# Row 0's Sinkhorn chains: reciprocals as a power of minus one on GpSimd

## The chip, the cores and the metric

The kernel runs on one core of one Trainium2 chip. A core has five engines that each execute their own list of instructions strictly in order: PE (matrix multiply), DVE (VectorE), ACT (ScalarE), POOL (GpSimd) and SP, which here only issues DMAs. They meet through semaphores. The metric is the device time of one execution in microseconds (us). Three runs of the kernel before gave 1398.83, 1407.75 and 1408.99 us; the median is 1407.75 us.

## The reference, cut to what matters

The model has two layers on an input of 2 batch rows of 512 tokens and 512 channels. Layer 0 is a gated linear attention and a feed-forward product, layer 1 a softmax attention and a mixing of four streams per token. The change touches only that last part. For every token a 4x4 matrix is made doubly stochastic by 50 Sinkhorn steps, which the reference does on logarithms:

```python
def sinkhorn_log(logits, num_iters=50, tau=0.1):
    Z = logits / tau
    u0 = jnp.zeros(Z.shape[:-1], Z.dtype)
    v0 = jnp.zeros_like(u0)
    def step(carry, _):
        u, v = carry
        u = -jax.nn.logsumexp(Z + v[..., None, :], axis=-1)
        v = -jax.nn.logsumexp(Z + u[..., :, None], axis=-2)
        return ((u, v), None)
    (u, v), _ = jax.lax.scan(step, (u0, v0), None, length=num_iters)
    return jnp.exp(Z + u[..., :, None] + v[..., None, :])
...
x_pre = jnp.einsum('btnc,btn->btc', x_streams, H_pre)
y = x_pre @ W_branch
x_mixed = jnp.einsum('btij,btjc->btic', H_res, x_streams)
y_distributed = jnp.einsum('btc,btn->btnc', y, H_post)
return (x_mixed + y_distributed).reshape(B, T, nC)
```

`H_res` is the result of `sinkhorn_log`, blended with the identity. A batch row ("row 0", "row 1") is one of the two entries of the first axis.

## The kernel before

The tokens stand 128 to a tile, so each batch row has four tiles. The first 1000 us or so are layer 0. Layer 1's attention (`maxima`, `weigh`, `outputs`, `finish`) follows in pieces of one kind after another; each finished pair of query tiles is handed to `streams(b, c0, n, last, ways)`, which does the final mixing for n = 2 tiles. There are four such calls. In the order of their start they are called A and B here (batch row 0, first and second half) and C and D (batch row 1). `last` is the entry of the constant `VECTOR = False, False, True, True`: it is false for A and B, true for C and D.

`streams` is a generator. After the norms and the small logits it carves its variables for the Sinkhorn steps out of one tile named `sinkhorn` (128 x 512): `z`, `K` and `t` hold two 4x4 matrices per partition (128 x 32), `fa` and `fb` the row and column factors (128 x 8). The first step is done with logarithms, the other 49 (`range(1, NITER)`) in plain numbers: multiply `K` by one factor (L1120 or L1124), add along one axis (`sums`), take the reciprocal (L1122 or L1126). One multiplication, sum and reciprocal is called a half-step here; a chain has 98 of them, each waiting for the one before. After steps 16 and 32 the factors are folded into the logarithms and `K` is formed anew with two Ln and one Exp on ACT and four additions on DVE.

Where `last` is true, all three operations are on DVE (`big = nc.vector`, one reduction in L1109). Where it is false, the multiplication is on POOL and the sum is two additions on POOL (L1112 and L1113, four to two to one); only the reciprocal is on DVE. So a half-step of A or B goes from POOL to DVE and back.

When a chain is done, DVE forms `hr` (L1135 to L1139) and each of the two tiles is mixed in one of three ways (`WAYS`): "tensor" (ACT makes diagonal matrices, PE multiplies, L1160 and L1161, DVE scales in L1165, POOL adds the residual in L1181), "gpsimd" (B's second tile: L1168, L1172, L1176, L1180, L1181 all on POOL) or "vector" (D's first tile, on DVE). A DMA then stores the tile.

The order of the instructions on each engine is fixed before the kernel runs. The source is traced in the order of the pieces; `aside(2)` advances each live `streams` generator by two `yield`s per piece, with a raised priority (`UPS`, 400). A planner then gives every engine its list from these priorities and from its own estimates of when an instruction will be ready. On the chip nothing is reordered: if the next instruction of an engine has to wait, all behind it wait too. POOL's list holds, beside the chains A and B, the attention's last two operations `o` and `xres` (L930, L932), which `streams` of the same tiles wait for. DVE's list holds the attention's maxima (L847) and the chains C and D beside the reciprocals of A and B.

Of the kernel before, what the change touches and what calls it, by code (L numbers as in the profile page):

```python
# [33 lines left out]
ALU = mybir.AluOpType  # L34
# [19 lines left out]
def tile_adaln(ctx: ExitStack, tc: tile.TileContext, a: dict, out: bass.AP):  # L54
    nc = tc.nc
# [11 lines left out]
    def act(o, i, func, **kw):  # L67
        ins = nc.scalar.activation(o, i, func, **kw)  # L68
        tc.add_manual_dep(
            ins.ins, table.ins.name,  # L70
            mybir.DependencyInfo(mybir.DependencyClass.NoSync, mybir.DependencyReason.DATA),
            reason="the activation table",
        )
        return ins.ins
# [80 lines left out]
    def bank(shape, name, bufs=2):  # L155
        return psp.tile(shape, FP, name=name, bufs=bufs)
# [810 lines left out]
    def streams(b, c0, n, last, ways):  # L967
# [87 lines left out]
        sh, sv = [P, n, NS, NS], [P, n, NS]  # L1055
# [6 lines left out]
        def carve(shape):  # L1062
            m = int(np.prod(shape[1:]))
            t = room[:, used[0]:used[0] + m]
            used[0] += m
            if len(shape) == 4:
                return t.rearrange("p (c i j) -> p c i j", i=NS, j=shape[3])
            return t.rearrange("p (c i) -> p c i", i=NS)
# [24 lines left out]
        fa, fb, fl = carve(sv), carve(sv), carve(sv)  # L1093
# [4 lines left out]
        def kernel_of():  # L1098
            nc.vector.tensor_tensor(K, z, over(u), ALU.add)
            nc.vector.tensor_tensor(K, K, along(v), ALU.add)  # L1100
            act(K, K, AF.Exp)
# [4 lines left out]
        def sums(dst, y):  # L1106

            if last:
                nc.vector.tensor_reduce(dst, y, AX.X, ALU.add)  # L1109
            else:  # L1110
                h2 = pairs
                nc.gpsimd.tensor_tensor(h2, y[:, :, :, 0:2], y[:, :, :, 2:4], ALU.add)  # L1112
                nc.gpsimd.tensor_tensor(dst, h2[:, :, :, 0], h2[:, :, :, 1], ALU.add)  # L1113

        fresh = True
        for it in range(1, NITER):
            if fresh:
                sums(fa, K)
            else:
                big.tensor_tensor(t, K, along(fb), ALU.mult)  # L1120
                sums(fa, t)
            nc.vector.reciprocal(fa, fa)  # L1122
            yield
            big.tensor_tensor(t, tp_(K), along(fa), ALU.mult)  # L1124
            sums(fb, t)
            nc.vector.reciprocal(fb, fb)  # L1126
            fresh = it in (16, 32)
            if fresh:
                for d, f in ((u, fa), (v, fb)):
                    act(fl, f, AF.Ln)  # L1130
                    nc.vector.tensor_tensor(d, d, fl, ALU.add)
                kernel_of()
            yield
# [6 lines left out]
        for c in range(n):  # L1140
            f = wts.tile([P, NS, P], FP, name="fout", bufs=2)
            ff = f.rearrange("p i c -> p (i c)")
            hv = h[c].rearrange("p (i c) -> p i c", i=NS)
            f4 = [P, NS, P]
            way = ways[c]
            if way == "vector":
                for i in range(NS):
                    nc.vector.tensor_scalar(f[:, i], yb[:, c, :], sm[:, c, 1, i:i + 1], None, ALU.mult)
                    for j in range(NS):
                        nc.vector.scalar_tensor_tensor(  # L1150
                            f[:, i], hv[:, j], hr[:, c, i, j:j + 1], f[:, i], ALU.mult, ALU.add
                        )
                    yield
            elif way == "tensor":
                mps = bank(f4, "mix")
                for i in range(NS):
                    dg = wts.tile([P, NS + 1, P], FP, name="dg", bufs=2)
                    for j in range(NS + 1):
                        w = hr[:, c, i, j:j + 1] if j < NS else sm[:, c, 1, i:i + 1]
                        nc.scalar.activation(dg[:, j], ident, AF.Copy, scale=w)  # L1160
                        nc.tensor.matmul(  # L1161
                            mps[:, i], lhsT=dg[:, j], rhs=hv[:, j] if j < NS else yb[:, c], start=j == 0, stop=j == NS
                        )
                    yield
                nc.vector.tensor_tensor(ff, mps.rearrange("p i c -> p (i c)"), rows1[b, GB], ALU.mult)  # L1165
            else:
                tj = wts.tile(f4, FP, name="tj", bufs=1)
                nc.gpsimd.tensor_tensor(  # L1168
                    f, yb[:, c, :].unsqueeze(1).to_broadcast(f4), sm[:, c, 1, :].unsqueeze(2).to_broadcast(f4), ALU.mult
                )  # L1170
                for j in range(NS):
                    nc.gpsimd.tensor_tensor(  # L1172
                        tj, hv[:, j].unsqueeze(1).to_broadcast(f4),
                        hr[:, c, :, j].unsqueeze(2).to_broadcast(f4), ALU.mult,
                    )
                    nc.gpsimd.tensor_tensor(f, f, tj, ALU.add)  # L1176
                    yield
            other = nc.vector if way == "vector" else nc.gpsimd
            if way != "tensor":
                other.tensor_tensor(ff, ff, rows1[b, GB], ALU.mult)  # L1180
            other.tensor_tensor(ff, ff, xs[c], ALU.add)  # L1181
            nc.sync.dma_start(out=out[(t0 + c) * P:(t0 + c + 1) * P, :], in_=ff)
            yield

    order = [
        {"b": b, "half": half, "t": t} for b in range(B) for half in range(2) for t in range(4)
# [53 lines left out]
    def weighed():  # L1240
        w = wt[0]
        wt[0] += 1
        if w < n_pieces:
            if w == n_pieces // 2:
                row_tiles(1, (GA,))
                values1(1)
            weigh(order[w // 8], w % 8)
        o = w - OUT
        if 0 <= o < n_pieces and o % 4 == 3:
            outputs(o // 4)  # L1250
        o -= 5
        if o >= 0 and o % 4 == 0 and o < n_pieces:
            j = o // 4
            finish(j)
            if j % 16 == 5:
                with behind():
                    row_tiles(j // 16, (SB, CB, GB))
                    weights24(j // 16)
            if j % 8 == 7:
                side.append((RATES[j // 8], streams(j // 16, j % 16 // 8 * 2, 2, VECTOR[j // 8], WAYS[j // 8]), UPS[j // 8]))  # L1260
# [170 lines left out]
```

## Time and profile before

The profiled execution took 1409.56 us, of which the span from the first to the last instruction is 1407.8 us.

| | busy in the span, us | share |
|---|---|---|
| PE | 1247.3 | 89% |
| DVE | 1164.4 | 83% |
| ACT | 825.1 | 59% |
| POOL | 787.2 | 56% |

| stretch, us from the start | PE busy | DVE busy | POOL busy | what is in it |
|---|---|---|---|---|
| 1111 to 1199 | 79.41 of 88 | 75.60 | 46.82 | attention, chain A |
| 1199 to 1265 | 62.38 of 66 | 55.48 | 39.63 | attention, A and B |
| 1265 to 1300 | 17.00 of 35 | 28.97 | 26.90 | A, B, C; D begins |
| 1300 to 1330 | 0.00 of 30 | 28.20 | 25.56 | all four chains |
| 1330 to 1370 | 11.99 of 40 | 37.51 | 23.89 | B, C, D; A is mixed |
| 1370 to 1390 | 17.45 of 20 | 16.47 | 9.24 | D; B and C are mixed |
| 1390 to 1408 | 7.92 of 18 | 14.63 | 9.24 | D is mixed |

An instruction's duration in these rows contains what it spends in the engine's pipeline, so neighbours on one engine overlap: 0.19 us instructions of DVE start 0.11 us apart where nothing makes them wait. A wait counts as idle time in front of an instruction, with the releaser beside it. A share over the whole span says little here, because the last 150 us have another limit than the rest.

### The profile page before, as it was taken

To read this page: it belongs to the slowest core of one execution; us is meant where nothing else is said; L and a number is where in the kernel's file an instruction comes from. 1 tells how busy PE (TensorE), PEld (TensorE's weight loads), DVE (VectorE), ACT (ScalarE), POOL (GpSimd) and SP (SyncE) were. 2 spreads that over 40 slices of the span, in tenths; PEclk is the share of its full clock that TensorE was granted. 3 is DMA by queue.
4 is the path that set the end of the run, shared out by engine and by line. 5 is a ranking of instruction groups with operands and counts; after the bars stand their busy time and mean duration, and the time that the engine had idled before them with its cause. 6 is when DMAs were issued, how large, how long until landed. Compare 5 with 4: busy or idle time off the path is not lost. (4 is left out here: it accounts for less than half of the span.)

```text
span 1407.8 us, 23038 instructions
## 1 busy us (share of the span) xinstructions
PE 1247.3 (89%) x7128; PEld 990.5 (70%) x7128; DVE 1164.4 (83%) x3171; ACT 825.1 (59%) x2333; POOL 787.2 (56%) x1180
## 2 busy tenths in 40 slices
PE   6979999999999999999988998899998899994117
PEld 3767888788788778888876777677776667762116
DVE  7998668687677687787999977788699879888998
ACT  5456576476476466666665655567567467653226
POOL 4363274365264367577777757644243644657854
PEclk9999999999999999999999999999999899986568
DMA  7121241231131233224333327623212331100001
GB/s 241 36 70 43 87 124 39 68 106 53 53 118 56 94 117 111 81 79 128 120 106 90 98 70 233 179 66 97 65 42 94 101 92 48 59 2 1 1 15 46
DMA packets 95378, 117.14 MB, mean 83 GB/s; under 512 B 10828, under 2 KB 50508, under 8 KB 95256
## 3 DMA queue, kind: packets, MB, share of 16 engines
q1 hardware_dynamic: 95256, 115.67, 27.6%
q8 instruction: 57, 0.93, 0.3%
q14 instruction: 65, 0.53, 0.1%
HBM read 102.11 MB, written 10.64 MB: 80 GB/s over the span
## 5 line engine op out<-in xcount | busy, mean ns | idle before, releaser
L847 DVE TENSOR_REDUCE m<-s 128x1 f32<-128x512 f32 x256 | 166.6, 673 | 21.8 <-PE s L843 21.5
L68 ACT ACTIVATE pt<-s 128x512 f32<-128x512 f32 x256 | 137.4, 601 | 33.1 <-PE s L877 31.5
L448 POOL TENSOR_TENSOR q<-xcos,rot 128x512 f32<-128x512 f32 x64 | 92.8, 1450 | 56.5 <-DVE xcos L446 52.5
L68 ACT ACTIVATE sg<-sg 128x512 f32<-128x512 f32 x128 | 80.7, 632 | 64.5 <-DVE sg L479 62.5
L496 POOL TENSOR_SCALAR_AFFINE_SELECT dec<-gb 128x512 f32<-128x512 f32 x64 | 48.3, 755 | 121.2 <-DMA gb<-g_dram 65.4
L843 PE MATMUL s<-ks,qs 96*128 96x512 f32 x256 | 104.9, 442 | 11.5 <-DVE m L847 7.6
L877 PE MATMUL s<-qs,ks 100*128 100x256 f32 x512 | 104.4, 309 | 10.2 <-DMA qs<-mm 6.8
L233 PE MATMUL pps<-hh,wq_h 128*128 128x512 f32 x256 | 103.3, 403 | 7.1 <-ACT vT L767 3.4
L877 PEld LDWEIGHTS s<-qs,ks 100*128 100x128 f32 x512 | 82.7, 199 | 32.8 <-issue 7.9
L68 ACT ACTIVATE dec<-dec,room 128x128 f32<-128x128 f32 x256 | 83.0, 398 | 34.8 <-POOL dec L496 34.6
L233 PE MATMUL ops<-wo_h,zh 128*128 128x512 f32 x256 | 102.2, 399 | 1.2 <-ACT zh L571 1.0
L233 PE MATMUL gps<-wg_h,hh 128*128 128x512 f32 x256 | 101.3, 398 | 1.5 <-ACT wg_h L210 1.2
L233 PE MATMUL ops<-wo_h,zl 128*128 128x512 f32 x256 | 101.5, 396 | 0.7 <-DVE zl L572 0.7
L233 PE MATMUL pps<-hl,wq_h 128*128 128x512 f32 x256 | 101.8, 398 | 0.0
L233 PE MATMUL pps<-hh,wq_l 128*128 128x512 f32 x256 | 101.5, 397 | 0.0
L233 PE MATMUL gps<-wg_l,hh 128*128 128x512 f32 x256 | 101.1, 395 | 0.0
L233 PE MATMUL ops<-wo_l,zh 128*128 128x512 f32 x256 | 100.6, 393 | 0.0
L233 PE MATMUL gps<-wg_h,hl 128*128 128x512 f32 x256 | 100.6, 393 | 0.0
L516 POOL TENSOR_TENSOR gb<-gb,q 128x512 f32<-128x512 f32 x48 | 62.3, 1299 | 60.3 <-ACT gb L68 46.7
L549 PE MATMUL yps<-v,dec 128*128 128x128 f32 x512 | 93.4, 278 | 2.7 <-DVE xcos L446 1.4
L555 ACT ACTIVATE z<-yps 128x128 f32<-128x128 f32 x256 | 67.5, 278 | 41.1 <-PE yps L551 30.5
L559 DVE SCALAR_TENSOR_TENSOR z<-yps,ss,sg 128x128 f32<-128x128 f32 x256 | 72.0, 340 | 22.5 <-ACT ss L68 22.3
(321 smaller groups left out, 3984.4 us busy)
## 6 DMA issues: line engine op xcount, KB each, us to landing
gb<-g_dram SPq DMA_DIRECT2D x64, 256.0 KB
raw<-in_wq SPq DMA_DIRECT2D x56, 256.0 KB
raw<-in_wg SPq DMA_DIRECT2D x48, 256.0 KB
raw<-in_wo SPq DMA_DIRECT2D x48, 256.0 KB
raw<-in_wmod SPq DMA_DIRECT2D x40, 256.0 KB
qs<-q_dram SPq DMA_DIRECT2D x64, 96.0 KB
q_dram<-hi SPq DMA_DIRECT2D x16, 256.0 KB
raw<-in_wk SPq DMA_DIRECT2D x14, 256.0 KB
```

What stands on the lines that cost most here:

```text
L68: ins = nc.scalar.activation(o, i, func, **kw)
L233: nc.tensor.matmul(ps, lhsT=l, rhs=r, start=i == 0, stop=i == n - 1)
L448: nc.gpsimd.tensor_tensor(dst, sp(xc_), sp(rot), ALU.add)
L496: anchor["pool"] = nc.gpsimd.affine_select(out=dec, in_=gb, pattern=[[0, REP0], [1, P]], compare_op=ALU.is_ge, fill=-1e30, base=0, channel ...
L516: nc.gpsimd.tensor_tensor(gb, gb, q[:, c], ALU.mult)
L549: nc.tensor.matmul(yps[:, h, :], lhsT=u["pr"][:, h, :], rhs=u["v"][:, c, :], start=True, stop=not c)
L555: nc.scalar.activation(z[:, h, :], yps[:, h, :], AF.Square, accum_out=ss[:, h:h + 1])
L559: nc.vector.scalar_tensor_tensor(z[:, h, :], yps[:, h, :], ss[:, h:h + 1], sg[:, h * P:(h + 1) * P], ALU.mult, ALU.mult)
L843: anchor["pe"] = nc.tensor.matmul(ps, lhsT=st["qs"][rp][0:KS, i, qt * P:(qt + 1) * P], rhs=st["ks"][s][0:KS], start=True, stop=True,).ins
L847: anchor["dve"] = nc.vector.tensor_reduce(st["m"][:, 2 * qt + s, i:i + 1], ps, AX.X, ALU.max, negate=True).ins
L877: nc.tensor.matmul(ps[:, j, :], lhsT=st["ks"][s][0:KM, kt * P:(kt + 1) * P], rhs=st["qs"][rp][0:KM, i, :], start=True, stop=True,)
```

## The change

The chains with `last` false (A and B) no longer use DVE for the reciprocal. A constant tile of minus one is written once per `streams` call, and POOL raises the factor, element by element, to that power. The chains C and D keep DVE's reciprocal. Nothing else in the kernel is edited.

```diff
+        minus1 = carve(sv)
+        nc.gpsimd.memset(minus1, -1.0)
+
+        def inverse(f):
+            if last:
+                nc.vector.reciprocal(f, f)
+            else:
+                nc.gpsimd.tensor_tensor(f, f, minus1, ALU.pow)
+
         fresh = True
         for it in range(1, NITER):
...
-            nc.vector.reciprocal(fa, fa)
+            inverse(fa)
             yield
             big.tensor_tensor(t, tp_(K), along(fa), ALU.mult)
             sums(fb, t)
-            nc.vector.reciprocal(fb, fb)
+            inverse(fb)
```

## The prediction

> **What bounds the kernel now.** I read the 40 slices first. In order: PE, DVE, POOL.
>
> ```profile
> PE   6979999999999999999988998899998899994117
> DVE  7998668687677687787999977788699879888998
> POOL 4363274365264367577777757644243644657854
> ```
>
> PE is the limit until about 1270 us; then it falls to 4, 1, 1 and DVE stands at 9. The end of the kernel is the Sinkhorn chains. Next the groups on the tile `sinkhorn` (minimum/median/maximum ns, first and last start):
>
> ```profile
> L1113 POOL TENSOR_TENSOR sinkhorn<-sinkhorn x196: 193/201/686, 1111.6 to 1370.5; 128x8 f32<-128x8 f32 x196
> L1122 DVE RECIPROCAL sinkhorn<-sinkhorn x196: 142/193/204, 1114.1 to 1387.8; 128x8 f32<-128x8 f32 x196
> L1126 DVE RECIPROCAL sinkhorn<-sinkhorn x196: 138/193/204, 1119.4 to 1389.0; 128x8 f32<-128x8 f32 x196
> ```
>
> A and B run on POOL from 1111 to 1370 us, C and D on DVE until 1389. Of 392 reciprocals, the 196 of A and B leave DVE. The timeline (start, duration) gives the pace. POOL, A and B interleaved, then B alone:
>
> ```profile
> 1301.97 0.21 POOL L1112 TENSOR_TENSOR sinkhorn<-sinkhorn 128x16 f32<-128x16 f32 x1
> ...
> 1303.28 0.21 POOL L1112 TENSOR_TENSOR sinkhorn<-sinkhorn 128x16 f32<-128x16 f32 x1
> ```
> ```profile
> 1331.08 0.24 POOL L1120 TENSOR_TENSOR sinkhorn<-sinkhorn 128x32 f32<-128x32 f32 x1 [0.32 <-DVE sinkhorn L1109]
> 1331.40 0.21 POOL L1112 TENSOR_TENSOR sinkhorn<-sinkhorn 128x16 f32<-128x16 f32 x1
> 1331.69 0.20 POOL L1113 TENSOR_TENSOR sinkhorn<-sinkhorn 128x8 f32<-128x8 f32 x1
> 1332.20 0.25 POOL L1124 TENSOR_TENSOR sinkhorn<-sinkhorn 128x32 f32<-128x32 f32 x1 [0.32 <-DVE sinkhorn L1122]
> ```
>
> Interleaved, six instructions (two half-steps) take 1.31 us: 0.65 per half-step, POOL nearly full (17.50 of 20 us busy in 1300 to 1320). Alone, a half-step takes 1.12 us, of which 0.51 passes between the start of the last addition and the next multiplication: 0.20 for the addition, the detour over DVE the rest. Last, DVE with D alone:
>
> ```profile
> 1374.43 0.19 DVE L1109 TENSOR_REDUCE sinkhorn<-sinkhorn 128x8 f32<-128x32 f32 x1
> 1374.65 0.20 DVE L1122 RECIPROCAL sinkhorn<-sinkhorn 128x8 f32<-128x8 f32 x1
> 1374.89 0.21 DVE L1124 TENSOR_TENSOR sinkhorn<-sinkhorn 128x32 f32<-128x32 f32 x1
> 1375.13 0.19 DVE L1109 TENSOR_REDUCE sinkhorn<-sinkhorn 128x8 f32<-128x32 f32 x1
> ```
>
> 0.70 us per half-step. From 1297 (D's start) to 1389, D takes 92 us for 98 half-steps, 0.94 each; the excess is other chains' work on a DVE that is busy 19.39 of 20 us in 1340 to 1360.
>
> **What leaves DVE.** 196 reciprocals at 0.19 us, 37 us of busy time, 0.11 us of pace each. 80 of them (as many as L1113 has there) lie in 1111 to 1265, beside a PE that is the limit (79.41 of 88 us busy until 1199): I give them 0 to 5 us. While D runs, it would fall towards 98 x 0.69 = 68 us, plus 3 us for two new formations of `K` and some 6 us for L1165 and for blocked multiplications: D would end near 1374 instead of 1389. DVE's gain is 15 us, 20 with the attention, if POOL lets it through.
>
> **What is added to POOL.** 196 powers on 128x8 (and four memsets; L828's take 0.13 us, and no one reads those of C and D). No row of this trace shows a power, so I call its time p and bound it. Lower end: the addition of the same shape, L1113, 0.20 us. The additions of 128x32, 128x128 and 128x512 take 0.24, 0.46 and 1.27 us: 2.1 ns per element on a floor of 0.19 us. I suppose that a power is worked out as a logarithm, a product and an exponential, in elementary steps that each cost what an addition does. With 100 of them at 2.1 ns for 8 elements it is 0.19 + 1.68 = 1.9 us, my upper end; the longest single instructions of POOL in this stretch, L211 with 1.73 and L670 with 1.70 us, are close to it. Between 0.2 and 1.9 I take 48 steps, p = 1.0 us: an estimate (two series of a dozen terms each, a multiplication and an addition per term), nearest to the 128x512 row. Below 0.2 nothing: no elementwise row of POOL is shorter at this shape.
>
> **The sum.** POOL's half-step becomes 0.65 + p interleaved. Alone it is 0.32 + 0.29 for multiplication and first addition, 0.29 to the power's start, p, and a 0.09 gap such as stands between dependent instructions above: 1.0 + p. Against 1.12 today, a chain alone is faster only for p under 0.13. So nothing is gained on POOL; only DVE's relief counts.
>
> With p = 1.0: between A's start at 1111 and B's at 1199, POOL has 46.8 us of work, 24.2 of it not the chains'. The remaining 63.8 us hold 63.8/2.0 = 32 half-steps of A, as many as today (L1113 has 32 there: today DVE's waits set the pace).
>
> ```profile
> POOL sinkhorn L1120 <- DVE sinkhorn L1126: 15.4, 15, 2.1
> POOL sinkhorn L1124 <- DVE sinkhorn L1122: 13.9, 13, 3.5
> ```
>
> (Who waits for whom in 1111 to 1265; us, times, longest. These waits are what goes, and p fills the place.) Then 66 half-steps of A beside 66 of B: 132 x 1.65 = 218 us. B's last 32 alone: 64 us. Other work of POOL after 1199 (L930, L932, L956, L1007 and A's L1181): 12 us. B ends at 1199 + 218 + 64 + 12 = 1493 instead of 1370. Then `hr` 1 us, B's second tile on POOL (L1168 1.04, four times 1.05 + 1.27, L1180 1.33, L1181 1.27: 12.9), another L1181, the store 3 us: 19 us with gaps. Span **1512 us**. The profiled execution lies 1.8 us above its span and 1.8 above the median, so the time on the median's scale is also **1512 us**.
>
> In general the end by POOL is 1294 + 2 x (98 - 63.8/(1 + p)) x (0.65 + p): p = 0.2 gives 1370, 0.42 gives 1408, 0.5 1422, 1.3 1568, 1.9 1680, 1.95 1690.
>
> [...]
>
> **What the longer POOL instruction does to DVE.** Two rows that overlap in time:
>
> ```profile
> 1338.68 1.27 POOL L1181 TENSOR_TENSOR fout<-fout,xres 128x512 f32<-128x512 f32 x1
> ```
> ```profile
> 1338.87 1.12 DVE L1120 TENSOR_TENSOR sinkhorn<-sinkhorn 128x32 f32<-128x32 f32 x1
> ```
>
> A 0.19 us multiplication on DVE lasts until POOL's addition ends. From 1381.26 to 1387.84, beside L1172, L1176 and L1181, D's half-step takes 1.25 instead of 0.69 us. If a power does the same to C and D, their common half-step is 0.69 + 2 x 0.56 = 1.8 us; D ends at 1297 + 98 x 1.8 = 1473, the kernel at 1492. Still under POOL's 1512, so it costs nothing there.
> [...]
>
> **Rivals.**
> 1. *The power is as cheap as an addition* (p under 0.35). POOL's end is then under 1396; D on DVE ends the kernel at 1408 - 15 = 1393, 1388 with the attention's share: **1390**. For it: DVE at 19.39 of 20 us and 196 instructions gone. Against it: a power is no single step. It decides from p below 0.42.
> 2. *POOL's list delays the attention.* L930 and L932 stand among the half-steps. By 1278, the attention's end, POOL's list holds 92 half-steps today and 34 us of other work; freed from DVE's waits, the planner may put 150 there. They take 150 x 1.65 + 34 = 282 us: the attention ends at 1393, 115 us late, and D starts at 1412. For the last 46 half-steps on POOL (76 us) D goes at 1.8 us, then 56 half-steps at 0.69: 1412 + 76 + 39 + 9 + 19 = **1555**. For it: POOL's order is fixed. Against it: the attention's pieces decide the priorities, and with today's 92 the lateness is 92 - 72 us of idle time = 20 us, which POOL's end covers.
> 3. *The power is far dearer*: two passes of 50 steps, **1680**; handled one element at a time, beyond all bounds here.
> 4. *It doesn't do what it says*: DVE is relieved but p near 0.42 gives it back: **1408**.
>
> **Numbers.** Chances by p: under 0.35 (rival 1) 0.12; 0.35 to 0.5 (rival 4, 1396 to 1422) 0.05; 0.5 to 1.3 (forecast, 1422 to 1568) 0.43, rival 2 taking 0.08 of it; 1.3 to 1.95 (rival 3's lower part, to 1690) 0.28; above 0.12. The likeliest is the forecast, 1512. A range from 1395 to 1700 leaves out about 0.08 below and 0.11 above. About 1% (14 us) is what a measurement of this kernel can tell from no change: faster needs under 1394, about 0.10; within 1% 0.07; slower 0.83.
>
> **What would show it.** Right: a new POOL group of 196 on 128x8, near 1.0 us; reciprocals L1122 and L1126 down to 98 each; POOL at 9 in the slices from 1200 on; the last chain made of POOL's power, sums and B's second tile; D done before B. [...] The size of p alone moves the time by some 170 us per microsecond; it is the weakest number here.

## The result and the profile after

The changed kernel takes **1639.83 us**, the median of four runs (1639.38 to 1640.27). The kernel before took 1406.32 us on the same chip, the median of four runs (1398.83 to 1408.99). The ratio is **1.167**, with a 95% interval of 1.1624 to 1.1717: 233.5 us slower. The profiled execution took 1640.27 us, its span is 1638.5 us.

The 40 slices of the changed kernel, each 41 us long:

```profile
PE   6889999999999999989897999999999100000206
...
DVE  7996777777768878899967986997888973000003
...
POOL 4453743635536676777665442448889999999985
```

In slices 31 to 38, from 1229 to 1557 us, POOL stands at 9. From slice 32 on PE is nearly idle beside it, and DVE falls to 0 from slice 35 on. In the kernel before it was DVE that stood at 8 and 9 at the end. The bound has moved from DVE to POOL, and the new bound lasts longer.

The groups on the tile `sinkhorn` (minimum/median/maximum ns, first and last start). The edit moves the lines: the power is L1122, the reciprocal of C and D is L1120, and the multiplications are L1129 and L1133.

```profile
L1113 POOL TENSOR_TENSOR sinkhorn<-sinkhorn x196: 192/203/761, 1110.5 to 1600.9; 128x8 f32<-128x8 f32 x196
L1122 POOL TENSOR_TENSOR sinkhorn<-sinkhorn x196: 1631/1647/1998, 1110.8 to 1601.1; 128x8 f32<-128x8 f32 x196
L1120 DVE RECIPROCAL sinkhorn<-sinkhorn x196: 151/203/206, 1254.8 to 1367.1; 128x8 f32<-128x8 f32 x196
```

There are 196 powers, of 1.65 us each, eight times a reciprocal on DVE. B's last sum moves from 1370.5 to 1600.9 us, 230 of the 233.5 us. D's last reciprocal moves the other way, from 1389.0 to 1367.1 us. So the change relieves DVE as it should, and nothing gains by it, because POOL ends later.

POOL's timeline (start, duration, both us) while A and B are interleaved, and then with B alone:

```profile
1400.60 1.65 POOL L1122 TENSOR_TENSOR sinkhorn<-sinkhorn 128x8 f32<-128x8 f32 x1
1402.22 0.20 POOL L1113 TENSOR_TENSOR sinkhorn<-sinkhorn 128x8 f32<-128x8 f32 x1
1402.38 0.25 POOL L1133 TENSOR_TENSOR sinkhorn<-sinkhorn 128x32 f32<-128x32 f32 x1
1402.58 1.63 POOL L1122 TENSOR_TENSOR sinkhorn<-sinkhorn 128x8 f32<-128x8 f32 x1
...
1404.88 1.65 POOL L1122 TENSOR_TENSOR sinkhorn<-sinkhorn 128x8 f32<-128x8 f32 x1
...
1574.93 1.65 POOL L1122 TENSOR_TENSOR sinkhorn<-sinkhorn 128x8 f32<-128x8 f32 x1
...
1577.55 1.65 POOL L1122 TENSOR_TENSOR sinkhorn<-sinkhorn 128x8 f32<-128x8 f32 x1
```

Two half-steps take 1404.88 - 1400.60 = 4.28 us, 2.14 each; over the whole stretch from 1300 to 1550 us there are 117 powers, which is the same. With B alone, a half-step takes 1577.55 - 1574.93 = 2.62 us. In both, the power is most of it.

### The profile page after: what moved, and what is told of

The parts are those of the page before. It is cut to its first block, busy times and chain, and to the rows that moved or that the text cites. A ratio compares the mean times of both kernels' runs of the same rounds, so it can differ in the third digit from the quotient of the medians.

```text
span 1638.5 us, 23082 instructions
## 1 busy us (share of the span) xinstructions
PE 1244.4 (76%) x7128; PEld 989.0 (60%) x7128; DVE 1140.4 (70%) x2975; ACT 825.5 (50%) x2333; POOL 1090.4 (67%) x1380
## 4 chain that ended last, share of the span: by engine, by line
PE 48%; POOL 23%; DVE 19%; DMA 4%; ACT 3%; issue 2%; SPq 0%; POOLq 0%; DVEq 0%; ACTq 0%
POOL sinkhorn L1122 15%; PE pps L233 12%; PE ops L233 8%; PE gps L233 7%; PE op L897 3%; DVE m L847 3%; PE yps L549 3%; PE s L877 2%; PE sps L233 2%; PE yps L551 2%; PE s L843 2%; POOL sinkhorn L1112 2%; POOL sinkhorn L1113 2%; PE cps L233 1%; PE mps L272 1%
## 5 line engine op out<-in xcount | busy, mean ns | idle before, releaser
L1122 POOL TENSOR_TENSOR sinkhorn<-sinkhorn 128x8 f32<-128x8 f32 x196 | 323.6, 1651 | 3.4
L1170 PE MATMUL mix<-h,dg 128*128 128x128 f32 x192 | 33.4, 322 | 304.5 <-ACT dg L1169 304.5
L1170 PEld LDWEIGHTS mix<-h,dg 128*128 128x128 f32 x192 | 29.8, 218 | 305.6 <-ACT dg L1169 305.6
L68 ACT ACTIVATE sinkhorn<-sinkhorn 128x8 f32<-128x8 f32 (+1 forms) x40 | 8.5, 220 | 207.4 <-POOL sinkhorn L1122 151.8
```

The costliest lines, as they stand in the source:

```text
L1122: nc.gpsimd.tensor_tensor(f, f, minus1, ALU.pow)
L1170: nc.tensor.matmul(mps[:, i], lhsT=dg[:, j], rhs=hv[:, j] if j < NS else yb[:, c], start=j == 0, stop=j == NS)
```

## The experiments

The theory is the prediction's own: POOL's chains set the end, the price p of the power sets their pace, and DVE's relief is worth some 15 us that only show if p is small. The runs were made on several chips; a time of the kernel before that stands beside a run is from the same chip. Each diff is against the changed kernel unless the text says otherwise, and stands in the branch of `inverse` for chains A and B. A time without a range is that of one run.

### An instruction of an addition's price in the power's place

```diff
-        nc.gpsimd.memset(minus1, -1.0)
+        nc.gpsimd.memset(minus1, 1.0)
...
-                nc.gpsimd.tensor_tensor(f, f, minus1, ALU.pow)
+                nc.gpsimd.tensor_tensor(f, minus1, minus1, ALU.mult)
```

> The power of A and B is replaced by a product of two tiles of ones of the same shape (128x8) on POOL, written over the factor; so the reciprocals of A and B are left out and the result is not the reference's. Everything else is the changed kernel. Theory 1 (the price of the power, 1.65 us an instruction, is the whole loss): the product costs 0.20 us like the addition, POOL is done with both chains near 1351 us, D on DVE near 1367 us, and the time is 1380 to 1395 us, 1 to 2% under the kernel before. Rival (the loss is POOL's fuller list and the order the planner makes of it, whatever the instruction costs): the time stays over 1450 us.

Measured: 1391.74 us (four runs, 1389.79 to 1393.55) against 1403.96 before, ratio 0.9913 (0.9895 to 0.9932). On its `sinkhorn` tile:

```profile
L1122 POOL TENSOR_TENSOR sinkhorn<-sinkhorn x196: 191/198/654, 1113.4 to 1348.6; 128x8 f32<-128x8 f32 x196
L1120 DVE RECIPROCAL sinkhorn<-sinkhorn x196: 143/197/204, 1253.9 to 1378.4; 128x8 f32<-128x8 f32 x196
```

With an instruction of 0.2 us there, B is done before 1349 us, 30 us before D, and D ends the kernel. This does two things. It leaves the power's own price, with what follows from it, as the cause of the 233 us: as many instructions stand on the same engine, and the rival's 1450 us are far off. And it shows the most that this move can bring with the rest of the kernel as it is: even with a reciprocal that costs POOL no more than an addition, the kernel would gain 0.9%.

The time is inside theory 1's range, but D isn't where theory 1 had it: its last reciprocal starts at 1378.4 us instead of near 1367. D starts at 1286.2, 11 us earlier than in the kernel before, and then takes 92 us, as long as there. The mixing behind B's end stands on POOL beside it, in operations over 128x512 of 1.04 to 1.28 us. DVE's multiplications from 1349 to 1379 us (busy us, mean ns | idle us before):

```profile
L1129 DVE TENSOR_TENSOR sinkhorn<-sinkhorn 128x32 f32<-128x32 f32 x14 | 7.2, 516 | 0.4
L1133 DVE TENSOR_TENSOR sinkhorn<-sinkhorn 128x32 f32<-128x32 f32 x14 | 6.1, 437 | 0.4
```

They take 0.52 and 0.44 us instead of 0.2, some 8 us in 28 half-steps. So what this run gains comes from D's earlier start, not from a faster D.

### Half of the power, and a quarter of it

```diff
-                nc.gpsimd.tensor_tensor(f, f, minus1, ALU.pow)
+                nc.gpsimd.tensor_tensor(f[:, 0:1], f[:, 0:1], minus1[:, 0:1], ALU.pow)
+                nc.gpsimd.tensor_tensor(f[:, 1:2], minus1[:, 1:2], minus1[:, 1:2], ALU.mult)
```

> Only the first tile's four factors of A and B are raised to the power (128x4); the second tile's four are overwritten by a product of ones, so half of the reciprocals of A and B are left out. Theory 1 (the power costs per element, 0.19 us plus 0.18 us for each): the 128x4 power takes 0.9 us and the kernel about 1530 us. Rival (the power has a fixed price per instruction, such as the entry into its code): 1.65 us again, and with the added product about 1667 us.

Measured: 1544.56 us, with 1.01 us for a power: a little over theory 1's 0.9 us and 1530 us, and far from the rival's 1.65 us and 1667 us. Then the quarter:

```diff
-                nc.gpsimd.tensor_tensor(f, f, minus1, ALU.pow)
+                nc.gpsimd.tensor_tensor(f[:, 0:1, 0:2], f[:, 0:1, 0:2], minus1[:, 0:1, 0:2], ALU.pow)
+                nc.gpsimd.tensor_tensor(f[:, 0:1, 2:4], minus1[:, 0:1, 2:4], minus1[:, 0:1, 2:4], ALU.mult)
+                nc.gpsimd.tensor_tensor(f[:, 1:2], minus1[:, 1:2], minus1[:, 1:2], ALU.mult)
```

> The power is taken of 2 of the 8 elements per partition only; the other 6 are set to one by two small products on GpSimd, so the output is not the reference's. Theory 1 (the price of the power is 0.38 us and 0.158 us per element of a partition, the line through the 128x4 and the 128x8 power): 0.70 us for one power; with 0.17 us for each product behind it the sum gives about 1520 us, 1505 to 1535. Rival (the price goes by groups of four elements): the 128x2 power takes 1.0 us like the 128x4 one, and the time is 1560 to 1590.

Measured: 1511.04 us, inside the 1505 to 1535 of theory 1, on a chip where the one run of the kernel before took 1413.29 us. The powers on the `sinkhorn` tile, first of the half and then of the quarter:

```profile
L1122 POOL TENSOR_TENSOR sinkhorn<-sinkhorn x196: 996/1013/1512, 1110.5 to 1506.4; 128x4 f32<-128x4 f32 x196
```
```profile
L1122 POOL TENSOR_TENSOR sinkhorn<-sinkhorn x196: 682/697/1164, 1107.6 to 1472.6; 128x2 f32<-128x2 f32 x196
```

Three points lie on one line: 0.697, 1.013 and 1.647 us for 2, 4 and 8 elements per partition. From two to four elements it is 0.158 us each, from four to eight 0.158 too, on a fixed part of 0.38 us. The price goes by the element, and the line through 128x8 and 128x4, drawn before the quarter was run, gave 0.70 us for 128x2. The time follows it, as the formula of the prediction says it should: with 0.17 us taken for each product it gives about 1545 us for the half and 1520 for the quarter.

### Chain A alone with powers

```diff
-                nc.gpsimd.tensor_tensor(f, f, minus1, ALU.pow)
+                if c0 == 0:
+                    nc.gpsimd.tensor_tensor(f, f, minus1, ALU.pow)
+                else:
+                    nc.vector.reciprocal(f, f)
```

> Only A's reciprocals go to POOL as a power, B's stay on DVE: 98 powers in place of 196. Theory 1 (POOL's list is the sum of its instructions): A has 23 half-steps by 1199 us as in the changed kernel, the other 75 at 2.14 us and B's 98 at 0.65 us fill POOL until 1199 + 161 + 64 + 12 = 1436 us, or 1447 us if B's last 23 run alone; with a tail of 36 us the kernel takes 1470 to 1485 us, 65 to 80 us over the kernel before. Rival (the loss is in B alone, the chain that ends last): under 1430 us.

Measured: 1490.34 us. On its `sinkhorn` tile:

```profile
L1123 POOL TENSOR_TENSOR sinkhorn<-sinkhorn x98: 1637/1647/1998, 1106.9 to 1425.9; 128x8 f32<-128x8 f32 x98
L1125 DVE RECIPROCAL sinkhorn<-sinkhorn x98: 138/202/204, 1197.0 to 1453.5; 128x8 f32<-128x8 f32 x98
```

Half of the powers cost 84 us over the 1406.08 before: less than half of 233, but far from free. B has no power of its own, and still its last reciprocal starts at 1453.5 instead of 1370.8 or so: B's multiplications and sums stand behind A's powers in POOL's list. The time is 5 us over the upper end expected, and B's end 6 us later than worked out.

### The reciprocals of A and B on ScalarE

```diff
-                nc.gpsimd.tensor_tensor(f, f, minus1, ALU.pow)
+                act(f, f, AF.Ln)
+                act(f, f, AF.Exp, scale=-1.0)
```

> The reciprocals of A and B leave DVE as in the change, but go to ACT as Ln and Exp with scale -1 (two instructions of 0.21 us). Theory 1 (DVE's relief is worth 15 to 20 us when it costs POOL nothing, and ACT is free beside the chains): D on DVE ends near 1367 us and the time is 1380 to 1395 us. Rival (an engine in order on the attention's path takes up the waits for POOL, now ACT instead of DVE): the attention ends later than 1278 us and the time is 1400 to 1430 us.

Measured: 1415.12 us (four runs, 1413.82 to 1418.15), ratio 1.0077 (1.0057 to 1.0097) to 1403.96 before. The time lies in the rival's range, but not for the rival's reason: the attention is not late, its last `xres` starts at 1268 us, 12 us earlier than before. D is done at 1364, as theory 1 had it. But B's chain ends at 1382, 11 us later than before, and the kernel ends as much later. POOL's timeline, with B alone:

```profile
1361.01 0.25 POOL L1134 TENSOR_TENSOR sinkhorn<-sinkhorn 128x32 f32<-128x32 f32 x1 [0.56 <-ACT sinkhorn L68]
...
1362.39 0.24 POOL L1130 TENSOR_TENSOR sinkhorn<-sinkhorn 128x32 f32<-128x32 f32 x1 [0.56 <-ACT sinkhorn L68]
```

A half-step over ACT takes 1.38 us where it took 1.12 over DVE: two dependent instructions of 0.2 us and the way there and back. DVE's relief shows in D's end and is given back by the slower chain B.

### Large products that have nothing to do with the chains

```diff
-                nc.gpsimd.tensor_tensor(f, f, minus1, ALU.pow)
+                nc.gpsimd.tensor_tensor(f, minus1, minus1, ALU.mult)
+                for q in range(2):
+                    nc.gpsimd.tensor_tensor(pad, pad, pad, ALU.mult)
```

Here `pad` is a 128x256 piece of the same tile, and the constant is one, as in the first experiment. This run and the next ask what a long instruction on POOL does to C and D on DVE.

> The power of A and B is replaced by a product of ones of the same shape and two products of ones over 128x256, together about 1.66 us of POOL that stream data all the time; the reciprocals of A and B are left out. Both theories: POOL is as full as with the power, the whole time about 1640 us. Theory S (POOL holds DVE's two-input operations only while it streams from memory, which the power hardly does): DVE's multiplications beside the products are stretched to 0.4 to 0.8 us and D ends after 1400 us, where it ended at 1367 us beside the power. Rival (long instructions of POOL do not hold small DVE operations in this phase at all): DVE's multiplications stay at 0.2 us and D ends near 1367 us.

Measured: 1509.4 us, and the expected time missed, because the load didn't stay where it was put. The products depend on nothing, so the planner moved half of them to the start of the kernel:

```profile
L1128 POOL TENSOR_TENSOR sinkhorn<-sinkhorn x392: 603/612/3193, 1.2 to 1382.2; 128x256 f32<-128x256 f32 x196
```

As a test of the total time it says nothing. D's last reciprocal came at 1399.2 us, 32 us later than beside the powers, but C's first had come 16 us later too. The next run ties the products to the chain.

### Streaming products of the power's length, tied to the chain

```diff
-                nc.gpsimd.tensor_tensor(f, f, minus1, ALU.pow)
+                for q in range(4):
+                    nc.gpsimd.tensor_tensor(pad, f.unsqueeze(1).to_broadcast([P, 16, n, NS]), ones_, ALU.mult)
+                nc.gpsimd.tensor_tensor(f, minus1, minus1, ALU.mult)
```

Both `pad` and `ones_` are pieces of 128x128, and the constant is one again; each product reads the factor, so it can't start before the chain is there.

> In the run e6_stream the planner moved the large products to the start of the kernel, since nothing tied them to the chain. Here four products over 128x128 read the factor (spread over 16 copies) before it is overwritten with ones, so they stand where the power stood: four times 0.46 us, streaming, in place of 1.65 us; the reciprocals of A and B are left out. Both theories: the kernel takes 1640 to 1720 us. Theory S (POOL holds DVE's operations with two inputs from SBUF while it streams; the power streams little and does not): DVE's multiplications of C and D rise to a mean of 0.3 us or more, and D's last one comes after 1390 us, where beside the power it came at 1367 us. Rival (POOL's business in general slows DVE or not, whatever it does): D ends near 1367 us again.

Measured: 1705.4 us, inside the range expected. D's last reciprocal came at 1380.5 us, 13 us later than beside the powers but 10 us earlier than theory S had it. DVE's multiplications of 128x32 from 1297 to 1360 us (busy us, mean ns | idle us before), first beside the powers in the changed kernel, then beside these products:

```profile
L1133 DVE TENSOR_TENSOR sinkhorn<-sinkhorn 128x32 f32<-128x32 f32 x65 | 13.7, 212 | 0.4
L1129 DVE TENSOR_TENSOR sinkhorn<-sinkhorn 128x32 f32<-128x32 f32 x61 | 12.2, 200 | 0.3
```
```profile
L1136 DVE TENSOR_TENSOR sinkhorn<-sinkhorn 128x32 f32<-128x32 f32 x57 | 18.9, 365 | 0.1
...
L1140 DVE TENSOR_TENSOR sinkhorn<-sinkhorn 128x32 f32<-128x32 f32 x60 | 16.9, 315 | 0.1
```

Two rows of each show why; the first two are of the changed kernel, the other two of this one:

```profile
1355.46 1.64 POOL L1122 TENSOR_TENSOR sinkhorn<-sinkhorn 128x8 f32<-128x8 f32 x1
1355.52 0.21 DVE L1133 TENSOR_TENSOR sinkhorn<-sinkhorn 128x32 f32<-128x32 f32 x1
```
```profile
1353.08 0.45 POOL L1128 TENSOR_TENSOR sinkhorn<-sinkhorn 128x128 f32<-128x128 f32 x1
1353.09 0.48 DVE L1140 TENSOR_TENSOR sinkhorn<-sinkhorn 128x32 f32<-128x32 f32 x1
```

A multiplication that starts 0.06 us into a power is done after 0.21 us, with 1.4 us of the power still to come. One that starts 0.01 us into a product of 0.45 us ends just after it, at 0.48. POOL is full in both stretches (62.84 and 63.00 of 63 us). So it isn't the length of POOL's instruction that holds DVE, but what it does in it: the products of 128x128 hold DVE's multiplications (means of 0.365 and 0.315 us), the powers of 128x8 don't (0.212 and 0.200 us).

### What makes up the end: C's and D's own buffers

The tail from B's last power to the end is 36 us, where the prediction had 19. All four `streams` calls share the buffers of `fout`, `dg` and `mix`. This edit, on top of the changed kernel, gives C and D buffers of their own:

```diff
-            f = wts.tile([P, NS, P], FP, name="fout", bufs=2)
+            f = wts.tile([P, NS, P], FP, name=f"fout{last:d}", bufs=2)
...
-                mps = bank(f4, "mix")
+                mps = bank(f4, f"mix{last:d}")
...
-                    dg = wts.tile([P, NS + 1, P], FP, name="dg", bufs=2)
+                    dg = wts.tile([P, NS + 1, P], FP, name=f"dg{last:d}", bufs=2)
```

> The changed kernel, but C and D have buffers of their own for the mixing (output tile, diagonal matrices, product). Theory T (the 36 us between B's last power and the end come from the mixing of C and D, which stands behind B's because they share B's buffers): C and D are mixed and stored soon after 1370, while B still runs; after B only its own two tiles are left, 19 to 25 us, and the time is 1622 to 1630 us; the powers stay at 1.65 us. Rival (the tail is B's own work, or the lists keep the order whatever the buffers): the tail stays 36 us, the time 1637 to 1643.

Measured: 1631.72 us, span 1629.9, 2 us above the range of theory T and 5 below the rival's; the one run of the kernel before on this chip took 1413.29 us, so the pieces below are read from the trace. Powers took 1.64 us. The groups of ACT behind B's end, first in the changed kernel (1603 to 1638.5 us), then here (1604 to 1630 us):

```profile
L1169 ACT ACTIVATE dg<-room,sinkhorn 128x128 f32<-128x128 f32 x64 | 20.1, 387 | 49.6 <-DVE sinkhorn L1148 47.3 <-PE mix L1170 2.3
L1169 ACT ACTIVATE dg<-room,sm 128x128 f32<-128x128 f32 x15 | 5.8, 386 | 0.0
```
```profile
L1169 ACT ACTIVATE dg<-room,sinkhorn 128x128 f32<-128x128 f32 x16 | 5.0, 386 | 47.6 <-DVE sinkhorn L1148 47.6
L1169 ACT ACTIVATE dg<-room,sm 128x128 f32<-128x128 f32 x3 | 1.2, 385 | 0.0
```

In the changed kernel, ACT still has some 80 diagonal matrices to make when B's chain is done: the 20 of B's first tile, and 60 of C and D, whose chains had been ready since about 1367 or earlier. With own buffers, some 20 are left. B's last power ends at 1605.3, and the tail is 24.6 us: 11 us of the 36 were the shared buffers. The rest is B's own, as theory T had it.

The same edit on the kernel before, on VectorE's reciprocals (the constant is still written, but not read):

> The kernel before, reciprocals on DVE, but the mixing of C and D has its own buffers (fout, dg, mix), so that it need not stand behind B's mixing in ACT's and PE's lists. Theory T (after B's end ACT has four tiles of diagonal matrices to make, 31 us, and that is one of two ends near 1405 us; the other is D on DVE): D's end at 1389 us still gives 1405 to 1410 us, no change. Rival (ACT's list alone sets the end): 1385 to 1395 us.

Measured: 1408.37 us (ten runs, 1405.10 to 1412.16) against 1406.08, ratio 1.0016 (1.0003 to 1.0028). That is theory T's range. There own buffers gain nothing: D's chain on DVE, with its last reciprocal at 1391.8 us, is late anyway.

And on ScalarE's reciprocals, where B's chain had ended 34 us before the kernel did:

> Reciprocals of A and B on ACT as in e5_act, and the mixing of C and D in its own buffers. Theory T (e5_act lost its relief of DVE because C's and D's mixing stood behind B's end at 1382 us in ACT's list): C and D are mixed before B ends, only B's own 18 us follow: 1395 to 1403 us, under the kernel before. Rival (the chains A and B are slower over ACT and that alone is the loss): 1412 us or more, like e5_act.

Measured: 1425.31 us (four runs, 1423.08 to 1427.14) against 1406.08, ratio 1.0133 (1.0113 to 1.0153): 19 us over the kernel before, where the shared buffers were 11 over it. Theory T missed, and the rival's range holds the time. The tail shrinks from 34 to 26 us (theory T had 18), but B's chain ends at 1400 instead of 1382. Who waits for whom on POOL from 1340 to 1382 us (us, times, longest):

```profile
POOL sinkhorn L1130 <- ACT sinkhorn L68: 11.0, 7, 5.5
POOL fout L1191 <- DVE fout L1175: 8.0, 5, 4.3
POOL sinkhorn L1134 <- ACT sinkhorn L68: 5.3, 6, 2.1
```

The mixing now comes earlier, and its diagonal matrices come into ACT's list, between the logarithms and exponentials of B: one wait for ACT lasts 5.5 us, where with shared buffers none was over 2.2. Its residual additions (L1191) come into POOL's list, between B's sums, and wait there for the mixing, 8.0 us where it was 1.1. In this stretch B gets through 16 half-steps, with shared buffers through 28.

### One chain on ScalarE

Both runs have own buffers for C and D, and only one chain's reciprocals on ACT; the other's stay on DVE:

```diff
-                nc.gpsimd.tensor_tensor(f, f, minus1, ALU.pow)
+                if c0 == 0:
+                    act(f, f, AF.Ln)
+                    act(f, f, AF.Exp, scale=-1.0)
+                else:
+                    nc.vector.reciprocal(f, f)
```

> Only chain A's reciprocals leave VectorE: they run on ScalarE as a logarithm and an exponential of minus it; B's stay on VectorE; C and D have buffers of their own for the mixing. Theory R (what counts is how much leaves VectorE without making B late): B's half-step is that of the kernel before, so B ends near 1370 or earlier, no Ln and Exp of A is left on ScalarE's list after about 1340, VectorE has 98 reciprocals (19 us of busy time) less, half of them while D runs, so D ends near 1379 instead of 1389, and the time is 1393 to 1400, a ratio of 0.991 to 0.996. Rival (ScalarE's list, as where both chains ran there): A's logarithms and exponentials stand between those of the attention and the diagonal matrices; A ends after 1360, B with it, and the time is 1405 to 1425.

Measured: 1405.19 us (ten runs, 1395.76 to 1410.00) against 1406.94 (thirteen runs), ratio 0.9975 (0.9947 to 1.0002). No difference is shown; theory R's 1393 to 1400 holds only the two fastest of the ten runs, 1395.76, which was the profiled one, and 1399.17. In the profiled one D's last reciprocal starts at 1379.9, near the 1379 worked out, although some of D's steps are held up. DVE and POOL there:

```profile
1371.20 0.20 DVE L1120 RECIPROCAL sinkhorn<-sinkhorn 128x8 f32<-128x8 f32 x1
1371.44 0.63 DVE L1137 TENSOR_TENSOR sinkhorn<-sinkhorn 128x32 f32<-128x32 f32 x1
1372.10 1.26 POOL L1189 TENSOR_TENSOR fout<-fout,tj 128x512 f32<-128x512 f32 x1
...
1372.57 0.84 DVE L1133 TENSOR_TENSOR sinkhorn<-sinkhorn 128x32 f32<-128x32 f32 x1
```

D's multiplications take 0.63 and 0.84 us instead of 0.2 while POOL mixes B's second tile. B is done early enough that its mixing falls beside D, and holds it. Why the other nine runs are 3 to 14 us longer isn't known.

And with the two branches exchanged:

```diff
-                nc.gpsimd.tensor_tensor(f, f, minus1, ALU.pow)
+                if c0:
+                    act(f, f, AF.Ln)
+                    act(f, f, AF.Exp, scale=-1.0)
+                else:
+                    nc.vector.reciprocal(f, f)
```

> The mirror image: only chain B's reciprocals run on ScalarE as a logarithm and an exponential of minus it, A's stay on VectorE, C and D have buffers of their own for the mixing. Theory R (what sets the end is B's last stretch, in which it runs alone): A's half-step is that of before, but B's last stretch alone costs 1.38 us per half-step over ScalarE instead of 1.12, with the diagonal matrices of C and D between its steps; B ends between 1375 and 1400, and the time is 1405 to 1425. Rival (VectorE's relief is all that counts, whichever chain it comes from): as with A on ScalarE, 1393 to 1400.

Measured: 1435.59 us (four runs, 1431.51 to 1437.23), ratio 1.0193 (1.0141 to 1.0245). Theory R had the direction, but 1405 to 1425: B's last sum starts at 1403.3, 3 us after the latest end that it gave B. The rival's 1393 to 1400 is far off, so it matters which chain is moved. That fits theory R's reason: A has the whole attention beside it, and B's last stretch stands in front of the end. No version here beats the kernel before by what can be measured, except the one that leaves the reciprocals out.

## Why the prediction was right or wrong

**The sign and the mechanism were right, the size was not.** 1512 us was predicted, 1639.83 measured.

**The term that was mis-sized is p**, "48 steps, p = 1.0 us". It measured 1.65 us. The step that failed is the count of 48: at 2.1 ns per step, the 0.158 us per element that the shapes show would be 75 steps, and the fixed part is 0.38 us where the addition's 0.19 was put. No row of the trace before bore on that count, and the bounds of 0.2 and 1.9 us said so. How the power is worked out inside isn't shown by any run: the 75 are only the price divided by 2.1 ns. The chance put on 1.3 to 1.95 us, where it lies, was 0.28 against 0.43 for the stretch chosen.

**The formula of the sum holds, partly by offsetting errors.** At p = 1.65 it gives 1294 + 2 x (98 - 24.1) x 2.30 = 1634 us; the span is 1638.5. Its pieces, as measured:

- Half-steps of A alone before 1199 us: 24 by the formula, 23 powers in the trace.
- Interleaved half-step: 0.65 + 1.65 = 2.30 by the formula, 2.14 in the trace. In the rows above an instruction starts some 0.04 us before the one ahead of it has ended, and the 0.65 held idle time of a POOL that wasn't full (17.50 of 20 us), which goes once it is. On some 150 half-steps that is 24 us too many.
- B alone: 1.0 + 1.65 = 2.65 by the formula, 2.62 in the trace. With an instruction of 0.2 us in the power's place, the formula gives 1.2, and the instructions L1122 of B alone there start at 1346.25, 1347.42 and 1348.61.
- B's end: 1615 by the formula, 1602.8 in the trace, 12 us earlier. Of the 24 us, some 9 went back to POOL's other work after 1199 us and its idle time while both chains run (15.8 and 5 us where 12 were given); the rest isn't accounted for piece by piece.
- The tail: 19 us by the formula, 35.7 in the trace. Only B's second tile was counted; the mixing of C and D behind it wasn't. Own buffers took 11 of the 17 us away. That tail was in the profile before too, 37 us from B's end at 1370.7 to 1407.8, beside D's own end. So the sum comes near 1638.5 by luck in part: B's end was put too late, and the tail too short.

**DVE's relief was right beside the powers.** D's end was put at 1374 us and came at 1367: D starts at 1287.7 instead of 1297.0, since the attention ends 7 us earlier (last `xres` 1274.1 instead of 1280.8; 0 to 5 us were given), and D then takes 79 us for 98 half-steps, where 77 were given. But this holds only because B, and with it the mixing on POOL, is late. Where B ended first, in the run with an instruction of 0.2 us, D took 92 us again.

**What the longer POOL instruction does to DVE was wrong.** The prediction worked out what follows if a power stretches DVE's multiplications by 0.56 us each, with D's end at 1473. They aren't stretched: their mean is 0.20 to 0.21 us beside the powers. (The 1.25 us that it read for D's half-step in the trace before is 1.22 by the rows from 1381.96 to 1388.07.) It cost the forecast nothing, because POOL was later anyway. The row it was read from, a multiplication of 1.12 us beside an addition of 128x512 of 1.27 us, was carried over to a power of 128x8. The products of 128x128 do hold a multiplication (0.48 us beside 0.45), the power doesn't (0.21 us inside 1.64).

**The rivals.** Rival 1 (a cheap power, 1390 us) fell by p. The run with an instruction of 0.2 us took 1391.74, so its sum came out, but by luck: it had a faster D, where D took 92 us as before, started 11 us earlier and had 13 us behind it instead of 19. Rival 2 (POOL's list delays the attention) fell: the attention ends earlier, and by 1278 us POOL has done 52 half-steps (23 before 1199 us, 29 after), not 150. Rival 3 (a dearer power, 1680) had the direction of the miss. Rival 4 (no effect, p near 0.42) fell by p.

## What to carry to other kernels

Before an operation is moved to an engine that has never run it in this kernel, its price there has to be measured, and one short run with it at two sizes gives it: here 0.38 us plus 0.158 us per element of a partition for GpSimd's power, against 0.2 us for VectorE's reciprocal of all eight. A first run with a cheap stand-in in the same place shows the most the move can bring, here 0.9%, and none of the real replacements tried here kept a part of it that could be measured. In the serial chains here it was the latency of a step that counted (B alone: 1.12 us per half-step over DVE, 1.38 over ACT, 2.62 with the power), and the relieved engine's busy time only where that engine ended last. And a chain that ends earlier starts the work behind it earlier, which can hold another one: here the mixing on POOL held D, whose multiplications took 0.44 to 0.52 us instead of 0.2.

## What the runs showed of the hardware that was not expected

- The power on GpSimd costs 0.697, 1.013 and 1.647 us on 128x2, 128x4 and 128x8 fp32: a straight line of 0.158 us per element.
- The first power takes 1.67 us, like the others: no delay of its own shows.
- A power of 1.64 us leaves DVE's operation with two inputs at 0.21 us; four products of 0.45 us in its place stretch its mean to 0.32 to 0.37 us. Why isn't settled by any run here.
- A logarithm and an exponential on ACT, at 0.2 us each, make a half-step of 1.38 us from POOL and back, 0.26 us more than the way over DVE with one reciprocal.
